# A decoder layer on one core: the query halves of twelve cross-attention tiles, moved from the feed-forward phase to the end of the self attention

## The chip, the cores and the metric

The kernel runs on one core of one Trainium2 chip. The core has a matrix engine (TensorE, "PE" in the profile, with "PEld" for its weight loads), a vector engine (DVE), an activation engine (ACT), a general engine (POOL, also GpSimd) and a sync engine (SP) that here only issues transfers. Each engine takes its instructions from its own queue in order and waits on semaphores for the others. The metric is the device time of one execution in microseconds (us). Three runs of the kernel before took 3417.92, 3418.64 and 3423.78 us, so the median is 3418.64 us.

## The reference, cut to what matters

The layer is a pre-norm decoder: self attention, cross attention and a feed-forward part that itself contains a grouped-query attention and a mixture of experts. `x` has four sequences of 512 tokens with 512 channels, all in float32.

```python
x = x + L0_attn(layernorm(x))          # gated delta rule, 16 heads of 128, causal convolutions
x = x + L0_xattn(layernorm(x), ctx)    # cross attention to 256 context rows, 16 heads of 32
x = x + L0_ffn(layernorm(x))           # 16 query heads, 4 key heads, then 8 experts, 2 per token
```

The change touches the second line:

```python
def L0_xattn(x, cond):
    q = (x @ Wq + bq).reshape(1, B * N, H, hd)
    k, v = ...                                   # of cond @ Wkv + bkv
    q = fq_sym(q * scale, axis=-1)               # round to 255 levels, one step per token and head
    k = fq_sym(k, axis=-1); v = fq_sym(v, axis=2)
    attn = softmax(einsum('bhqd,bhkd->bhqk', q, k))
    attn = fq_unsigned(attn, axis=-1)            # 256 levels, one step per row
    out = einsum('bhqk,bhkd->bhqd', attn, v)
    return out @ Wp + bp
```

## The kernel before, in words

**Tiles.** The 2048 tokens are 16 tiles of 128 rows (`NT`), four to a sequence (`TB`). The self attention works by groups `m` of two heads of one sequence, 32 in all; the later parts work by token tile.

**Streams.** Nearly everything is written as Python generators. A generator issues a few instructions and yields. `turns` (L192) steps several streams round by round, each by a given number of steps; `chain` puts streams one after another; `within` stops a stream for now when the turn is over; `idle(n)` yields n times. So the order in which instructions are written comes from how streams are stepped against each other. In the self attention, DVE, ACT and POOL execute exactly in that written order (L1066, `manual_schedule`); the order on TensorE and of the transfers on SP is chosen by the framework's scheduler, with the written order as priority. After the self attention the scheduler chooses for all engines.

**Self attention.** Turn `m` runs `stage3(m)` (L829), which joins the blocks of an inverse (four steps: L843 to L877) and then runs the recurrence over four chunks: `r` (DVE, L897), `u` (TensorE L904, ACT L906), new state (TensorE L914, DVE L919), output (L922, L924). That makes 15 steps. Each step of it steps the other streams of the turn once or twice: `stage1(m+2)` (keys and queries two groups ahead), `stage2_values(m+1)` (convolutions), the inversion by POOL (L747, L748, 31 rounds) and `output(m-1)` (the projection of the group before, L968). In the last two turns, 30 and 31, there is no stage 1 left, and in turn 31 no convolutions and no inversion either. When `stage3` is through, what is left of the other streams is run off.

**Cross attention of tile i** has two halves. `front(i)` (L244 to L280) loads the tile's rows `x1d` (after self attention) into `xi`, normalizes them (DVE L140, L141, L131, then a power on POOL L132, then DVE L146), transposes them (TensorE L215, copied by ACT L217), projects them (L259, eight matmul instructions), adds the bias (DVE L261), quantizes them (`levels`, seven DVE instructions, L225 to L232; the step per head stays in `x_step`), transposes the bfloat16 levels, stores them in DRAM (`x_q_d`), and reads them back in four transfers with each head's rows three times (`x_qT`, L279). That is 11 steps, or 9 where `xi` was loaded ahead. `back(i)` (L283) makes scores for four heads at a time (L296), their maxima and exponentials (DVE L300 to L302, ACT L306), rounds them (DVE L312), transposes them (L322), weights the values (`weighted`, L328) and projects the result (L364): 14 steps, four scores and roundings, four transposes, two `weighted`.

**Where the halves run.** In turn 30 the streams `front(0)` and `front(1)` start, one step per step of `stage3`; front 0 is done in it. In turn 31 the stream `seam`, two steps at a time, finishes front 1 beside back 0 and continues with `cross(1)`, which is front 2 and back 1. Back 1 gets as far as its second scores. The rest of it runs in the seam (L1606) beside `output(31)` and `norms(0)`.

**The weave.** From there `weave` (L155) merges four kinds of streams by due times: `attention(i)`, `qkv(i)` (projections with weights streamed from DRAM, L1253), `crossing(i)` and `rest_of(i)`. Of all streams, the one whose time is earliest is stepped, and its time advances by its length divided by its expected number of steps (`steps`, L152). `crossing(i)`, for i from 2 to 15, is the norm of tile i-1 beside the first six steps of `cross(i)`, and then the rest of it; `cross(i)` (L370) is front i+1 and then back i. Its streams have due times 3.1 tiles ahead (`X`) with a length of 1.03 (`W`). After the weave the expert blocks run.

**Memory.** The pool `wx` (name `b_x`) holds what both halves of the cross attention need, with single buffers for `xi`, `xn` and `x_qi`; `wz` (`b_v`) is opened in turn 31. The pool `second` is closed at the start of turn 31, and only then the keys and weights of back (`x_kT`, `wpj`, `bp`, `x_val`) are loaded on SP (L1099 to L1104).

Of the kernel before, what the change touches and what calls it, by code (L numbers as in the profile page):

```python
# [31 lines left out]
F32 = mybir.dt.float32  # L32
BF16 = mybir.dt.bfloat16
# [6 lines left out]
P = 128  # L40
# [64 lines left out]
def decoder(ctx: ExitStack, tc: tile.TileContext, a: dict, out: bass.AP):  # L105
# [42 lines left out]
    def chain(*gs):  # L148
        for g in gs:
            yield from g  # L150

    steps = {"first_o": 3, "cross": 30, "qkv": 12, "rest_of": 4, "route": 10, "load": 26}  # L152
    steps.update((f"attention{c}", n) for c, n in enumerate((37, 41, 53, 57)))
# [24 lines left out]
    def idle(n):  # L178
        for _ in range(n):
            yield  # L180
# [6 lines left out]
    def within(g, turn):  # L187

        while turn and next(g, g) is not g:
            yield  # L190
# [45 lines left out]
    x_kT_d, x_val_d = dram.tile([P, 3, KD, M], BF16, name="x_kT_d"), dram.tile([P, 2, D], BF16, name="x_val_d")  # L236
    x_q_d = dram.tile([NT, P, KD, P], BF16, name="x_q_d")

    ao = ctx.enter_context(tc.tile_pool(name="a_o", bufs=2))
    top = ctx.enter_context(ExitStack())  # L240

    hTs, x2s, xis, fronts = {}, {}, {}, {}

    def front(i):  # L244

        xi = xis.pop(i, None)
        if xi is None:
            xi = wx.tile([P, D], F32, name="xi", bufs=1)
            nc.sync.dma_start(xi, x1d[i])
            yield  # L250
            yield
        xn = wx.tile([P, D], F32, name="xn", bufs=1)
        yield from layernorm(xn.unsqueeze(1), xi.unsqueeze(1), wx)
        yield
        xT = transposed(xn, wx, "xT")
        yield
        pq = p_b.tile([P, D], F32, name="pb")
        for kd in range(KD):
            nc.tensor.matmul(pq, xT[:, kd, :], wq[:, kd, :], start=kd == 0, stop=kd == KD - 1)  # L259
        q = wx.tile([P, D], F32, name="xn", bufs=1)  # L260
        nc.vector.tensor_tensor(q, pq, bq, ALU.add)  # L261
        yield
        qi = wx.tile([P, D], BF16, name="x_qi", bufs=1)
        step = wx.tile([P, H2], F32, name="x_step")
        levels(qi, q, step, H2, HD2, wx, float(1.0 / np.sqrt(np.float32(HD2))))
        yield
        yield
        t = transposed(qi, wx, "x_qi", 1)
        yield

        nc.sync.dma_start(x_q_d[i], t)
        if 1 < i + 1 < NT:
            xis[i + 1] = wx.tile([P, D], F32, name="xi", bufs=1)
            nc.sync.dma_start(xis[i + 1], x1d[i + 1])
        yield
        qT = wx.tile([3 * HD2, KD, 4, P], BF16, name="x_qT")
        for r in range(4):
            q = x_q_d[i, r * HD2 : (r + 1) * HD2].unsqueeze(0).to_broadcast([3, HD2, KD, P])
            nc.sync.dma_start(qT[:, :, r, :], q)  # L279
        yield  # L280
        fronts[i] = qT, step

    def back(i):  # L283

        qT, step = fronts.pop(i)
        aT = wx.tile([P, KD, P], F32, name="xT")
# [62 lines left out]
        for u in range(5):  # L349
            if i == 0 and u < KD:  # L350
                nc.gpsimd.tensor_scalar(wpj[:, u, :], wpj[:, u, :], x_sv[:, u : u + 1], None, ALU.mult)
            if u == 3:
                x2 = wz.tile([P, D], F32, name="x2", bufs=2)
                nc.sync.dma_start(x2, x1d[i])
            if u < 4:
                yield from scores(u // 2 * 2, u % 2 * 2, es)
            if u > 0:
                yield from turned(es.pop(0), eTs)
            if u in (2, 4):
                yield from weighted(u - 2, eTs)  # L360
                eTs.clear()
# [6 lines left out]
        x2s[i] = x2  # L368

    def cross(i):  # L370
        return chain(front(i + 1), back(i)) if i + 1 < NT else back(i)


    with ExitStack() as st:
# [707 lines left out]
        for m in range(NP):  # L1082
            rest, turn = [], [0]
            if m == NP - 2:
# [5 lines left out]
                wx = top.enter_context(tc.tile_pool(name="b_x", bufs=2, side="right", reuse_waits="tile"))  # L1090
                fronts_of = chain(idle(2), front(0), front(1))
                rest.append((within(fronts_of, turn), 1))
            if m == NP - 1:
# [11 lines left out]
                wz = top.enter_context(tc.tile_pool(name="b_v", bufs=2, side="right", reuse_waits="tile"))  # L1105
                seam = chain(turns((fronts_of, 1), (chain(idle(3), back(0)), 1)), cross(1))
                rest.append((within(seam, turn), 2))
# [30 lines left out]
    with ExitStack() as st:  # L1138
# [38 lines left out]
        def norms(i):  # L1177


            x2 = x2s.pop(i)  # L1180
            x3 = wq_.tile([P, D], F32, name="x3", bufs=1)
# [404 lines left out]

        at_x = [(2 - X + (i - 2) * W, W, crossing(i), "cross") for i in range(2, NT)]
        for n, t in enumerate((-0.6, 0.2, 1.0)):
            at_x[n] = (t, 0.8, *at_x[n][2:])
        at_x[-1] = (*at_x[-1][:2], last(chain(at_x[-1][2], norms(NT - 1))), "cross")  # L1590
        at_q = [(i - Q, 1.0, qkv(i), "qkv") for i in range(NT)]
# [5 lines left out]
        for i in range(NT - 1):  # L1597
# [172 lines left out]
```

## Time and profile before

| | us |
|---|---|
| median of three runs | 3418.64 |
| the profiled execution | 3410.54 |
| its span (first to last instruction) | 3408.8 |
| busy: TensorE | 3207.6 (94%) |
| busy: DVE | 1831.8 (54%) |
| busy: ACT | 1606.2 (47%) |
| busy: POOL | 1448.0 (42%) |
| turn 30 begins (its first L843) | 1752.8 |
| turn 31 begins (its first L843) | 1798.3 |
| `output(31)` begins after the last `og` | 1872.7 |
| first matmul of `qkv(0)` (L1253) | 1906.9 |
| last matmul of the feed-forward attention (L1359) | 3130.7 |

The stages of the self attention before turn 30 and the weave take nearly the whole span. Busy times are sums over one engine; matmuls are pipelined and their ends are modelled, so the time that a group of matmuls takes is read from the start of the first to the start of what follows. The mean granted TensorE clock of the execution was 0.976 of full speed. In the rows of the timeline, the bracket at the end of a line is how long the engine was idle before it, and what ended that.

### The profile page before, as it was taken

How to read it: one execution, taken by the hardware profiler on the slowest of the kernel's cores; microseconds unless marked ns; L12 is line 12 of the kernel's file. 1: busy time of each engine (PE TensorE's matmuls, PEld its weight loads, DVE VectorE, ACT ScalarE, POOL GpSimd, SP SyncE). 2: the span in 40 equal slices, each digit the busy share in tenths (PEclk: the TensorE clock that was granted, in tenths of full speed). 3: DMA queues.
4: the chain of work that ended last, by engine and by line, in shares of the span. 5: the costliest groups of instructions: out<-in, count | busy, mean ns of one | idle time of the engine just before them, and what ended most of it. 6: DMA issues, size and time to landing. Idle time of an engine off the chain costs nothing. (4 is left out here: it accounts for less than half of the span.)

```text
span 3408.8 us, 48178 instructions
## 1 busy us (share of the span) xinstructions
PE 3207.6 (94%) x16031; PEld 1796.9 (53%) x16031; DVE 1831.8 (54%) x4160; ACT 1606.2 (47%) x4384; POOL 1448.0 (42%) x2768
## 2 busy tenths in 40 slices
PE   5899999999999999999997799999998999899996
PEld 3455555555555555555554355555554555454443
DVE  5755564555645555554554466666655665545111
ACT  3445555455545555445543445555544455534221
POOL 1156756667576675766761221112112111212442
PEclk8999999999999999999997899999999999999998
DMA  6443444534345353444532565556545554556544
GB/s 173 114 122 111 136 109 124 161 114 134 111 124 152 113 147 104 125 138 122 141 98 75 194 201 178 160 176 182 170 158 159 189 164 148 169 164 225 93 81 95
DMA packets 491288, 482.05 MB, mean 141 GB/s; under 512 B 224911, under 2 KB 340117, under 8 KB 490848
## 3 DMA queue, kind: packets, MB, share of 16 engines
q1 hardware_dynamic: 477696, 448.79, 44.2%
q0 software_dynamic: 11904, 27.34, 3.9%
q8 instruction: 128, 2.10, 0.3%
q10 hardware_dynamic: 1440, 2.84, 0.3%
q14 instruction: 120, 0.98, 0.1%
HBM read 416.18 MB, written 66.90 MB: 142 GB/s over the span
## 5 line engine op out<-in xcount | busy, mean ns | idle before, releaser
L594 PE MATMUL pb<-xnT,w 128*128 128x512 f32 x2048 | 958.0, 603 | 0.1
L594 PEld LDWEIGHTS pb<-xnT,w 128*128 128x128 f32 x2048 | 364.1, 192 | 337.2 <-issue 330.7
L605 DVE SCALAR_TENSOR_TENSOR cv<-pb,pp,cv 128x510 f32<-128x510 f32 (+2 forms) x576 | 424.3, 746 | 98.8 <-ACT cv L602 85.6
L748 POOL TENSOR_TENSOR iT<-iT,iW 64x126 f32<-64x126 f32 (+22 forms) x930 | 343.3, 369 | 72.9
L1253 PE MATMUL pb<-c_q,hT 128*128 128x512 f32 x768 | 354.4, 599 | 5.0 <-DMA c_q<-in_c_wq_dram 3.8
L747 POOL TENSOR_TENSOR iW<-iA,iT 64x126 f32<-64x126 f32 (+22 forms) x930 | 319.7, 344 | 65.7 <-issue 0.2
L968 PE MATMUL pb<-wot,og 128*128 128x512 f32 x512 | 248.3, 608 | 11.3 <-ACT x_e L306 6.3
L1172 POOL TENSOR_TENSOR rope_s<-q,tab 128x128 f32<-128x128 f32 x80 | 43.1, 538 | 477.1 <-DVE q L1283 392.2
L1253 PEld LDWEIGHTS pb<-c_q,hT 128*128 128x128 f32 x768 | 141.7, 192 | 156.9 <-issue 146.7
L602 ACT ACTIVATE cv<-pb,pp 128x512 f32<-128x512 f32 x192 | 148.5, 773 | 147.6 <-PE pb L594 143.6
L649 POOL TENSOR_TENSOR rk<-ss,mhalf 128x8 f32<-128x8 f32 x32 | 77.9, 2435 | 277.0 <-DVE ss L648 277.0
L973 DVE TENSOR_TENSOR xa<-pb,xa 128x512 f32<-128x512 f32 x112 | 76.9, 688 | 188.1 <-PE pb L968 188.1
L306 ACT ACTIVATE x_e<-pb,nm,x_step 128x256 f32<-128x256 f32 x256 | 141.1, 565 | 70.2 <-DVE nm L302 60.6
L1349 PE MATMUL po<-eT,val 128*128 128x512 f32 x320 | 165.6, 614 | 7.6 <-ACT eT L1347 4.7
L1359 PE MATMUL pw<-wot,oT 128*128 128x512 f32 x344 | 163.9, 601 | 0.4 <-DVE oT L1351 0.2
L1319 PE MATMUL pb<-kT,qT 128*128 128x256 f32 (+3 forms) x576 | 161.9, 409 | 0.0
L701 POOL TENSOR_TENSOR qg<-qh,row 128x512 f32<-128x512 f32 x64 | 83.2, 1300 | 177.7 <-ACT qh L608 154.8
L968 PEld LDWEIGHTS pb<-wot,og 128*128 128x128 f32 x512 | 92.8, 192 | 106.4 <-issue 88.0
L1660 PE MATMUL pb<-w_gu,eT 128*128 x312 | 141.9, 598 | 2.0 <-issue 2.0
L608 ACT ACTIVATE qh<-cv 128x512 f32<-128x512 f32 x64 | 40.4, 631 | 214.0 <-DVE cv L605 206.1
L132 POOL TENSOR_TENSOR rms_r<-rsq,mhalf 128x1 f32<-128x1 f32 x48 | 27.4, 571 | 243.9 <-DVE rsq L131 243.8
L1347 ACT COPY eT<-pb 128x512 f32<-128x512 f32 x160 | 89.4, 592 | 82.9 <-PE pb L1345 80.1
(389 smaller groups left out, 6184.1 us busy)
## 6 DMA issues: line engine op xcount, KB each, us to landing
c_q<-in_c_wq_dram SPq DMA_DIRECT2D x128, 512.0 KB
w<-in_a_w_dram SPq DMA_DIRECT2D x124, 512.0 KB
wot<-in_c_wo_dram SPq DMA_DIRECT2D x86, 512.0 KB
row<-g_d SPq DMA_DIRECT2D x64, 512.0 KB
c_o<-in_c_wo_dram SPq DMA_DIRECT2D x42, 512.0 KB
at_d<-at SPq DMA_DIRECT2D x64, 256.0 KB
T<-t_d SPq DMA_DIRECT2D x32, 512.0 KB
X<-x_d SPq DMA_DIRECT2D x32, 512.0 KB
```

What stands on the lines that cost most here:

```text
L306: nc.scalar.activation(e[:, 2 * r + g, :], ps[r][:, g, :], AF.Exp, bias=nm[:, r, g : g + 1], scale=step[:, h : h + 1], accum_out=ssum[:, g ...
L594: nc.tensor.matmul(pj, wt[:, kd, p * P : (p + 1) * P], xnT[:, kd, :], start=kd == 0, stop=kd == KD - 1)
L602: nc.scalar.activation(ac, pj, AF.Identity, bias=cb[:, m, h : h + 1], scale=cw[:, m, h, 3:4])
L605: nc.vector.scalar_tensor_tensor(ac[:, j:], pj[:, : S - j], cw[:, m, h, 3 - j : 4 - j], ac[:, j:], ALU.mult, ALU.add)
L747: eng.tensor_tensor(u, A[:, i, i + 1 :].unsqueeze(2).to_broadcast([nb, n, w]), T[:, i, :w].unsqueeze(1).to_broadcast([nb, n, w]), ALU.mult)
L748: eng.tensor_tensor(T[:, i + 1 :, :w], T[:, i + 1 :, :w], u, ALU.add)
L968: nc.tensor.matmul(pw, og[p][:, c * P : (c + 1) * P], wot[:, p, :], start=p == 0, stop=p == HG - 1)
L1253: nc.tensor.matmul(pj, hT[:, kd, :], w[:, kd % 2, :], start=kd == 0, stop=kd == KD - 1)
L1319: nc.tensor.matmul(ps[:, m, k * P : (k + w) * P], qT[g][:, n + m, :], kT[:, g, j : j + w, :], start=True, stop=True)
L1349: nc.tensor.matmul(po, val[:, g, :], eT, start=k == 0, stop=k == c)
L1359: nc.tensor.matmul(pw, oT[:, h + m, :], w[:, m, :], start=g == 0 and h + m == 0, stop=g == 3 and h + m == 3)
L1660: nc.tensor.matmul(pg, hT[:, kd, :], w_gu[:, bass.ds(e, 1), kd, :, :], start=kd == 0, stop=kd == KD - 1)
```

## The change

The fronts of tiles 0 to 11 no longer run in the weave. Tiles 0, 1, 2, 4, 5, 7, 8, 9, 10 and 11 form one stream, `fronts_of`, which is stepped twice per step of `stage3` in turns 30 and 31 and once per round in the seam, until it ends. Fronts 3 and 6 are streams of their own, in turn 30 and in turn 31, with a small pool each (`x_more`). A front of `fronts_of` loads the next front's rows once its own are normalized, so all but the first have 8 steps in place of 11.

A front now ends by storing its levels in `x_q_d` and its steps in a new DRAM tensor `x_s_d`. Reading them back is a new function, `fetch`, with the four transfers of before and one for the steps. `back(i)` calls it for tile i+1 at its third part if that front is done, or at its own start for tile i. `x_qT` moves from the pool `wx` to `wz`.

The seam stream is only back 0 and back 1, two steps per step of `stage3` in turn 31. In the weave, `crossing(2)` to `crossing(10)` and `crossing(15)` hold only the back (kind "back", 20 steps expected); `crossing(11)` to `crossing(14)` hold fronts 12 to 15 as before. `norms(i)` waits until tile i's cross attention is written.

```diff
-    steps = {"first_o": 3, "cross": 30, "qkv": 12, "rest_of": 4, "route": 10, "load": 26}
+    steps = {"first_o": 3, "cross": 30, "back": 20, "qkv": 12, "rest_of": 4, "route": 10, "load": 26}
...
-    x_q_d = dram.tile([NT, P, KD, P], BF16, name="x_q_d")
+    x_q_d, x_s_d = dram.tile([NT, P, KD, P], BF16, name="x_q_d"), dram.tile([NT, P, H2], F32, name="x_s_d")
...
-    def front(i):
-
-        xi = xis.pop(i, None)
-        if xi is None:
-            xi = wx.tile([P, D], F32, name="xi", bufs=1)
-            nc.sync.dma_start(xi, x1d[i])
+    def front(i, pool=None, then=None):
+        pool = pool or wx
+
+        def load(n):
+            xis[n] = pool.tile([P, D], F32, name="xi", bufs=1)
+            nc.sync.dma_start(xis[n], x1d[n])
+
+        if i not in xis:
+            load(i)
             yield
             yield
...
+        if then is not None:
+            load(then)
...
         nc.sync.dma_start(x_q_d[i], t)
-        if 1 < i + 1 < NT:
-            xis[i + 1] = wx.tile([P, D], F32, name="xi", bufs=1)
-            nc.sync.dma_start(xis[i + 1], x1d[i + 1])
+        nc.sync.dma_start(x_s_d[i], step)
+        fronts.add(i)
         yield
-        qT = wx.tile([3 * HD2, KD, 4, P], BF16, name="x_qT")
+
+    def fetch(i):
+        qT = wz.tile([3 * HD2, KD, 4, P], BF16, name="x_qT")
         for r in range(4):
             q = x_q_d[i, r * HD2 : (r + 1) * HD2].unsqueeze(0).to_broadcast([3, HD2, KD, P])
             nc.sync.dma_start(qT[:, :, r, :], q)
-        yield
-        fronts[i] = qT, step
+        step = wz.tile([P, H2], F32, name="x_step")
+        nc.sync.dma_start(step, x_s_d[i])
+        queries[i] = qT, step

     def back(i):

-        qT, step = fronts.pop(i)
+        if i not in queries:
+            fetch(i)
+            yield
+            yield
+        qT, step = queries.pop(i)
...
+            if u == 2 and i + 1 in fronts:
+                fetch(i + 1)
...
+    AHEAD = 3 * TB
+
     def cross(i):
-        return chain(front(i + 1), back(i)) if i + 1 < NT else back(i)
+        return chain(front(i + 1), back(i)) if AHEAD <= i + 1 < NT else back(i)
...
-                fronts_of = chain(idle(2), front(0), front(1))
-                rest.append((within(fronts_of, turn), 1))
+                more = second.enter_context(tc.tile_pool(name="x_more", bufs=1))
+                mine = (0, 1, 2, 4, 5, 7, 8, 9, 10, 11)
+                fronts_of = chain(idle(2), *(front(i, None, then) for i, then in zip(mine, (*mine[1:], None))))
+                rest.append((within(fronts_of, turn), 2))
+                rest.append((chain(idle(4), front(3, more)), 1))
...
-                seam = chain(turns((fronts_of, 1), (chain(idle(3), back(0)), 1)), cross(1))
+                more = st.enter_context(tc.tile_pool(name="x_more", bufs=1))
+                rest.append((chain(idle(2), front(6, more)), 1))
+                rest.append((within(fronts_of, turn), 2))
+                seam = chain(back(0), back(1))
                 rest.append((within(seam, turn), 2))
...
+            while i not in x2s:
+                yield
             x2 = x2s.pop(i)
...
-        at_x = [(2 - X + (i - 2) * W, W, crossing(i), "cross") for i in range(2, NT)]
+        at_x = [(2 - X + (i - 2) * W, W, crossing(i), "cross" if AHEAD <= i + 1 < NT else "back") for i in range(2, NT)]
...
-        run(turns((output(NP - 1), 1), (norms(0), 1), (seam, 1)))
+        run(turns((output(NP - 1), 1), (norms(0), 1), (seam, 1), (fronts_of, 1)))
```

More of the change, by code (lines that the diff above doesn't have):

```diff
@@ L236, in decoder @@
     x_kT_d, x_val_d = dram.tile([P, 3, KD, M], BF16, name="x_kT_d"), dram.tile([P, 2, D], BF16, name="x_val_d")
-    x_q_d = dram.tile([NT, P, KD, P], BF16, name="x_q_d")
+    x_q_d, x_s_d = dram.tile([NT, P, KD, P], BF16, name="x_q_d"), dram.tile([NT, P, H2], F32, name="x_s_d")
     ao = ctx.enter_context(tc.tile_pool(name="a_o", bufs=2))
     top = ctx.enter_context(ExitStack())
-    hTs, x2s, xis, fronts = {}, {}, {}, {}
-    def front(i):
-        xi = xis.pop(i, None)
-        if xi is None:
-            xi = wx.tile([P, D], F32, name="xi", bufs=1)
-            nc.sync.dma_start(xi, x1d[i])
+    hTs, x2s, xis, queries, fronts = {}, {}, {}, {}, set()
+    def front(i, pool=None, then=None):
[5 more added lines that the diff above has]
+            load(i)
             yield
             yield
-        xn = wx.tile([P, D], F32, name="xn", bufs=1)
-        yield from layernorm(xn.unsqueeze(1), xi.unsqueeze(1), wx)
+        xi = xis.pop(i)
+        xn = pool.tile([P, D], F32, name="xn", bufs=1)
+        yield from layernorm(xn.unsqueeze(1), xi.unsqueeze(1), pool)
         yield
-        xT = transposed(xn, wx, "xT")
+        if then is not None:
+            load(then)
+        xT = transposed(xn, pool, "xT", 2 if pool is wx else 1)
         yield
@@ L259, in front @@
             nc.tensor.matmul(pq, xT[:, kd, :], wq[:, kd, :], start=kd == 0, stop=kd == KD - 1)
-        q = wx.tile([P, D], F32, name="xn", bufs=1)
+        q = pool.tile([P, D], F32, name="xn", bufs=1)
         nc.vector.tensor_tensor(q, pq, bq, ALU.add)
         yield
-        qi = wx.tile([P, D], BF16, name="x_qi", bufs=1)
-        step = wx.tile([P, H2], F32, name="x_step")
-        levels(qi, q, step, H2, HD2, wx, float(1.0 / np.sqrt(np.float32(HD2))))
+        qi = pool.tile([P, D], BF16, name="x_qi", bufs=1)
+        step = pool.tile([P, H2], F32, name="x_step")
+        levels(qi, q, step, H2, HD2, pool, float(1.0 / np.sqrt(np.float32(HD2))))
         yield
         yield
-        t = transposed(qi, wx, "x_qi", 1)
+        t = transposed(qi, pool, "x_qi", 1)
         yield
         nc.sync.dma_start(x_q_d[i], t)
-        if 1 < i + 1 < NT:
-            xis[i + 1] = wx.tile([P, D], F32, name="xi", bufs=1)
-            nc.sync.dma_start(xis[i + 1], x1d[i + 1])
+        nc.sync.dma_start(x_s_d[i], step)
+        fronts.add(i)
         yield
-        qT = wx.tile([3 * HD2, KD, 4, P], BF16, name="x_qT")
+    def fetch(i):
+        qT = wz.tile([3 * HD2, KD, 4, P], BF16, name="x_qT")
         for r in range(4):
@@ L1585, in decoder @@
         Q, X, W = 1.36, 3.1, 1.03
-        at_x = [(2 - X + (i - 2) * W, W, crossing(i), "cross") for i in range(2, NT)]
+        at_x = [(2 - X + (i - 2) * W, W, crossing(i), "cross" if AHEAD <= i + 1 < NT else "back") for i in range(2, NT)]
         for n, t in enumerate((-0.6, 0.2, 1.0)):
             at_x[n] = (t, 0.8, *at_x[n][2:])
-        at_x[-1] = (*at_x[-1][:2], last(chain(at_x[-1][2], norms(NT - 1))), "cross")
+        at_x[-1] = (*at_x[-1][:2], last(chain(at_x[-1][2], norms(NT - 1))), "back")
         at_q = [(i - Q, 1.0, qkv(i), "qkv") for i in range(NT)]
```

## The prediction

> **What bounds the kernel now.** I read the page first for the share of each engine and for where in the span it changes, then the busy time by stage around the change, then the order of instructions and the waits inside those stages. Part 2 of the page, 40 slices of 85 us, TensorE and its granted clock:
>
> ```profile
> PE   5899999999999999999997799999998999899996
> PEclk8999999999999999999997899999999999999998
> ```
>
> TensorE is full nearly everywhere, except in slices 22 and 23 (1790 to 1960 us): the last two turns of the self attention and the seam. The busy time by stage shows it sharper. The stages are cut at the first matmul of turn 30, of turn 31, of `output(31)`, at the first projection of the feed-forward attention (L1253), and at 1960 us, after which the weave runs evenly; columns are TensorE, its weight loads, DVE, ACT and POOL, granted clock, DMA share, GB/s:
>
> ```profile
> core 0: us, PE busy (x) PEld busy (x) DVE busy (x) ACT busy (x) POOL busy (x), PEclk, DMA share, GB/s
> 1752.80:1798.30 45.50, 39.58 (x237) 23.81 (x236) 19.84 (x39) 12.74 (x34) 25.20 (x53) 0.92 0.36 103
> 1798.30:1872.70 74.40, 50.76 (x313) 31.07 (x312) 38.55 (x88) 28.63 (x83) 16.11 (x16) 0.78 0.27 80
> 1872.70:1906.90 34.20, 22.86 (x112) 11.87 (x113) 17.72 (x46) 13.04 (x34) 9.99 (x14) 0.67 0.68 237
> 1906.90:1960.00 53.10, 42.04 (x188) 22.21 (x187) 26.53 (x66) 24.22 (x68) 10.12 (x17) 0.87 0.51 161
> 1960.00:3125.00 1165.00, 1123.41 (x4731) 612.00 (x4730) 701.44 (x2003) 587.72 (x1566) 207.63 (x313) 0.99 0.56 178
> ```
>
> The weave is bound by TensorE: 1123.4 of 1165 us (96%) at clock 0.99, DVE at 60%. Turn 31 is bound by nothing: TensorE idles 23.6 us, DVE 35.9 us. There a chain over engines sets the pace, since DVE, ACT and POOL take their work strictly in the written order. One passage of front 0 in turn 30 shows what that costs. TensorE, from the timeline:
>
> ```profile
> 1770.44 0.60 PE L215 MATMUL pb<-tab,xn 128*128 128x128 f32 x4
> 1770.88 1.88 PE L594 MATMUL pb<-xnT,w 128*128 128x512 f32 x4
> ...
> 1773.04 3.60 PE L259 MATMUL pb<-wq,xT 128*128 128x512 f32 x8
> 1776.47 0.61 PE L914 MATMUL ps<-u,kdec 128*128 128x128 f32 x4
> ...
> 1784.64 0.80 PE L904 MATMUL ps<-r,X 128*128 128x128 f32 x2 [4.77 <-DVE r L897]
> ```
>
> and DVE in the same stretch:
>
> ```profile
> 1776.68 0.69 DVE L261 TENSOR_TENSOR xn<-pb,bq 128x512 f32<-128x512 f32 x1 [5.65 <-PE pb L259]
> ...
> 1779.24 0.68 DVE L225 TENSOR_REDUCE x_step<-xn 128x16 f32<-128x512 f32 x1
> ...
> 1783.24 0.43 DVE L232 TENSOR_SCALAR x_qi<-xn 128x512 bf16<-128x512 f32 x1
> ...
> 1784.24 0.60 DVE L897 SCALAR_TENSOR_TENSOR r<-ps,ngam,vn 128x128 f32<-128x128 f32 x2
> ```
>
> DVE first waits 5.65 us for the projection, then works off the quantization (`levels`), and only then the recurrence's `r`; TensorE stands 4.77 us for it. In turn 31 the DVE waits repeat the pattern (us in total, times, longest):
>
> ```profile
> DVE xn L261 <- PE pb L259: 10.4, 2, 7.3
> DVE x_ei L312 <- ACT x_e L306: 5.7, 3, 2.4
> DVE ln_st L140 <- DMA xi<-x1d: 4.4, 2, 2.7
> ```
>
> **What a front costs.** TensorE, by starts: 0.44 (f32 transposes, 1770.44 to 1770.88) + 3.43 (projection, 1773.04 to 1776.47) + 0.42 (bf16 transposes) = 4.29 us. DVE by the medians of its lines: 0.69 + 0.18 + 0.15 + 0.55 + 0.69 + 0.69 + 0.17 + 0.25 + 0.17 + 0.69 + 0.43 + 0.43 = 5.09 us. ACT: two copies of 0.58. POOL: one power of 0.55.
>
> **Weave.** Fronts 3 to 11 leave it, nine: 9 x 4.29 = **-38.6 us**. It stays bound by TensorE, as DVE loses work too. Bounds: -40 (divided by 96%) and -25, if its 41.6 us of idle grow by a third because the fronts no longer fill them.
>
> **Turn 30.** It carries front 0 now; by counting steps (two per step of `stage3`, one for front 3) it will carry 0, 1, 2 and 3. Three more: 12.9 us of TensorE. The turn has 5.9 us of TensorE idle, so at least +7. At most each new front also stalls the recurrence by 4.8 us as front 0 did: 12.9 + 14.3 = +27. Their `levels` fall in steps 4, 10 and 12, apart from each other, with step 8 stalling as now; so I take two stalls less a few us of filled idle: 12.9 + 9.5 - 2.4 = **+20**. POOL gets three more powers among the inversion's pairs (0.85 us a pair). The inversion ended at 1779.6 and its loads were issued by 1783.2 for a use at 1798.3, so 15 us cover that; without them it would cost 1.7.
>
> **Turn 31.** It carries fronts 1 and 2, back 0 and two scores of back 1. After: fronts 4 to 8, back 0, and back 1 but for its projection. DVE adds 3 x 5.1 for fronts, and for back 1 another 7.1 (two scores of 1.6, three roundings of 0.69, two `weighted` of 0.9): +22.4 us. Lowest is 0, since new TensorE work (12.9 + 3.9 = 16.8) is less than the 23.6 idle. Highest: the DVE work in full, three waits for projections at their mean (5.2) and three for exponentials (2.4): 22.4 + 15.6 + 7.3 = +45. The row nearest is the turn's own start, where a front and a back ran together: the inverse's steps started at 1801.6, 1813.9 and 1822.1, 10 us a step, against 4.2 where only back 0 ran (1822.1 to 1847.2, six steps). After the change all 15 steps carry both. So I lie near the top: 22.4 + 3 x 3.08 (the smaller projection wait) + 2 x 2.4 = **+36**. On SP, tile 0's queries are now fetched in turn 31, behind `x_kT` (6.14 us of issuing), `wpj`, `bp` and `x_val`: last of four issued about 1811.3, landed some 2.7 us later (as `xi`, issued 1852.57, was used at 1855.25), 2.4 us after the first scores ran now (1811.6); DVE and ACT stand behind those scores. That lies in the 36. In POOL the power of front 5 stands behind the scaling of `wpj` (6.2 us now), again inside the bounds.
>
> **Seam, 1872.7 to 1906.9.** TensorE holds 22.9 us at clock 0.67. Back 1 leaves all but its projection (3.9 us less); fronts 9 to 11 come (12.9) and fill idle time. The stage ends when the first projection's weights, issued from 1877.5 on, are in and TensorE is past back 1. DMA runs at 0.84 to 0.92 up to 1900, so at most 10 us can go: **-6**, bounds -10 and +13 (no cover at all). In 1906.9 to 1960 TensorE idles 11.1 us, partly behind back 1 and tile 1's norm, which come earlier: **-2**, bounds -11 and 0.
>
> **Steps through DRAM.** Each tile gains a store and a load of 8 KB, each about 0.33 us of SP issue (as the 4 KB `r_d` store, 0.32), beside 6.14 us for the query's loads that were there. SP has gaps; nothing on the path: 0. If the cover went, 0.7 x 16 = 11 us. [...]
>
> **Sum.** 20 + 36 - 6 - 2 - 38.6 = **+9.4 us**. The profiled execution took 3410.54 us (span 3408.8 and 1.7 around it), 8 under the median of three runs, 3418.64; it would become 3419.9, and the median **3428.0**.
>
> The granted clock could give back more: 0.78 in turn 31, 50.8 us busy, so at most 50.8 x 0.22 = 11 us. I take none, since the waits of 2.4 to 7.3 us remain. [...]
>
> **Rivals.** With G the growth of both turns (56 forecast), the time is 3418.6 + G - 46.6.
> - *Fronts fill idle TensorE.* For it: 29.5 us idle in the two turns, and fronts of two pools that overlap. Against: the waits are DVE's, in order. Its bound, G = 7, gives 3379; around G = 22, 3394. It decides below G = 40: faster by over 0.2%.
> - *Even.* G of 40 to 53: 3412 to 3425, within 0.2% (6.8 us, about what a measurement of this kernel can tell from no change).
> - *The weave gives back less.* TensorE waits there for `x_ei` (6.8), `h` (6.5) and `c_q` (3.8); if the missing fronts leave holes (-25 for -38.6): 3442, with G at its bound of 72, 3458.
> - *The change does nothing*, since TensorE's work is only moved: 3418.6. The stages differ too much in their idle time for more than chance to make it even; it counts within the even case.
>
> **Numbers.** Forecast case, G 53 to 75, 3425 to 3447: 0.43. Fill: 0.28. Even: 0.17. Less back, above 3447: 0.12. So faster 0.28, same 0.17, slower 0.55. The range 3396 to 3450 leaves out about a tenth at each end.
>
> **What would show it.** Turn 30 (from the first L843 of group 30 to that of group 31) at 65 us and turn 31 at 110; TensorE waiting there for `r`, `x_ei` and `xn`; clock still under 0.9. First L1253 about 28 us after `og`. The weave from there to the last L1359 shorter by 35 to 40 us. I am wrong if the turns grow by less than 40 us, or if the weave keeps its length.

## The result, and the profile after

The change made the kernel slower: 3448.88 us (median of 4 runs, 3445.81 to 3451.13) against 3418.47 us (4 runs, 3417.92 to 3423.78), a ratio of 1.0085 with a 95% interval of 1.0067 to 1.0102, or +30.4 us. Forecast were +9.4 us, a median of 3428.0 and a range of 3396 to 3450. The profiled execution after took 3445.81 us, span 3444.0.

Part 2 of the page of the changed kernel, TensorE in 40 slices of 86 us; the dip stands where it stood before, in slices 22 and 23, and is no shallower:

```profile
PE   5899999999999999999997699999998999899996
```

The busy time by stage of the changed kernel, cut at the first matmul of turn 30, of turn 31, of `output(31)` (1934.26), at the first projection of the encoder (L1281, L1253 before) and at the last `L1387` (L1359 before):

```profile
core 0: us, PE busy (x) PEld busy (x) DVE busy (x) ACT busy (x) POOL busy (x), PEclk, DMA share, GB/s
1756.30:1816.80 60.50, 52.67 (x285) 29.43 (x284) 35.14 (x78) 15.96 (x40) 27.67 (x57) 0.97 0.30 90
1816.80:1934.30 117.50, 73.23 (x438) 44.29 (x437) 58.31 (x136) 41.60 (x114) 16.50 (x17) 0.77 0.27 73
1934.30:1981.30 47.00, 32.49 (x84) 15.38 (x85) 25.17 (x67) 6.03 (x13) 13.29 (x19) 0.79 0.54 185
1981.30:3163.60 1182.30, 1137.15 (x4791) 618.23 (x4789) 683.12 (x1965) 602.25 (x1616) 212.25 (x320) 0.99 0.57 180
```

The last three of these stages in the kernel before, on the same marks (its first `output(31)` matmul is at 1873.83, which moves that cut by 1.1 us against the prediction's):

```profile
1798.30:1873.80 75.50, 50.76 (x313) 31.07 (x312) 39.65 (x89) 29.73 (x87) 16.11 (x16) 0.78 0.27 79
1873.80:1906.90 33.10, 22.86 (x112) 11.87 (x113) 16.62 (x45) 11.94 (x30) 9.99 (x14) 0.68 0.69 243
1906.90:3130.70 1223.80, 1171.02 (x4934) 636.87 (x4933) 729.85 (x2072) 612.19 (x1633) 217.75 (x330) 0.99 0.56 177
```

So the stages compare as follows:

| stage, us | before | after | difference | forecast |
|---|---|---|---|---|
| turn 30 | 45.5 | 60.5 | +15.0 | +20 |
| turn 31 | 75.5 | 117.5 | +42.0 | +36 |
| seam | 33.1 | 47.0 | +13.9 | -6 |
| woven stretch | 1223.8 | 1182.3 | -41.5 | -40.6 |
| seam and woven stretch together | 1256.9 | 1229.3 | -27.6 | -46.6 |

Before turn 30 and after the weave the two executions differ by another 5.8 us. The start of turn 30 alone lay between 1753.1 and 1756.8 us in kernels that are the same up to there, so these are not counted.

TensorE's idle time tells it most shortly. In turn 31 the kernel before idled 24.7 us (75.5 less 50.76); the changed one, with five fronts and most of back 1 in it, idles 44.3 (117.5 less 73.23). The added work did not go into the idle time, it brought more along. In seam and weave together TensorE idled 63.0 us before (10.2 and 52.8) and 59.7 after (14.5 and 45.2), so little idle time was filled there either. The waits of TensorE in turn 31 of the changed kernel (us in total, times, longest):

```profile
PE pb L352 <- DVE x_by L349: 7.9, 3, 4.1
PE pb L267 <- ACT xT L217: 5.1, 2, 4.2
PE pb L215 <- ACT x_e L321: 5.1, 2, 2.6
PE pb L311 <- DMA x_qT<-x_q_d: 5.0, 2, 3.3
PE pb L988 <- DVE og L955: 4.8, 1, 4.8
PE po L942 <- ACT u L926: 3.8, 1, 3.8
```

There is no one cause: backs (L352), fronts (L267, L215), the fetched queries (L311) and the recurrence (L942, L988) take turns in being late. VectorE waits the other way round, for TensorE's projections (10.4 us before) and for ScalarE's exponentials (5.7 us before):

```profile
DVE xn L269 <- PE pb L267: 22.0, 5, 7.8
DVE x_ei L327 <- ACT x_e L321: 13.0, 5, 3.8
```

The seam is where the forecast had the wrong sign. TensorE's timeline of the changed kernel from the second `output(31)` part on:

```profile
1947.07 3.60 PE L267 MATMUL pb<-wq,xT 128*128 128x512 f32 x8
1950.51 0.60 PE L1224 MATMUL pb<-tab,h 128*128 128x128 f32 x4
...
1956.80 0.61 PE L215 MATMUL pb<-ident_i,x_qi 128*128 128x128 bf16 x4 [4.91 <-DVE x_qi L232]
1957.47 1.09 PE L215 MATMUL pb<-tab,xn 128*128 128x128 f32 x4
1959.23 5.15 PE L267 MATMUL pb<-wq,xT 128*128 128x512 f32 x8 [0.68 <-ACT xT L217]
1968.30 0.40 PE L215 MATMUL pb<-ident_i,x_qi 128*128 128x128 bf16 x4 [3.92 <-DVE x_qi L232]
...
1970.80 6.18 PE L267 MATMUL pb<-wq,xT 128*128 128x512 f32 x8 [0.68 <-ACT xT L217]
1980.91 0.61 PE L215 MATMUL pb<-ident_i,x_qi 128*128 128x128 bf16 x4 [3.92 <-DVE x_qi L232]
1981.31 4.58 PE L1281 MATMUL pb<-c_q,hT 128*128 128x512 f32 x5
```

Fronts 9, 10 and 11 go one after the other, about 12 us apart (1947.07, 1959.23, 1970.80), each a bare chain: projection, then VectorE's quantization, then the bf16 transposes for which TensorE stands 4 to 5 us. The first projection of the encoder needs `hT`, whose transposes are at 1950.51, and weights whose loads were issued by 1940.6. It could start then (in kernel 10 below it starts at 1951.04), but it stands in TensorE's queue behind all three fronts, until 1981.31.

### The profile page after: what moved, and what is told of

Its sections match the earlier page's. It is cut to its first block, busy times and chain, and to the rows that moved or that the text cites. A ratio compares the mean times of both kernels' runs of the same rounds, so it can differ in the third digit from the quotient of the medians.

```text
span 3444.0 us, 48299 instructions
## 1 busy us (share of the span) xinstructions
PE 3222.1 (94%) x16031; PEld 1802.1 (52%) x16031; DVE 1827.7 (53%) x4160; ACT 1606.3 (47%) x4384; POOL 1452.3 (42%) x2768
## 5 line engine op out<-in xcount | busy, mean ns | idle before, releaser
L1281 PE MATMUL pb<-c_q,hT 128*128 128x512 f32 x768 | 356.6, 603 | 6.8 <-DVE q L1297 4.1
L988 PE MATMUL pb<-wot,og 128*128 128x512 f32 x512 | 249.5, 611 | 9.8 <-DVE og L955 4.8
L1281 PEld LDWEIGHTS pb<-c_q,hT 128*128 128x128 f32 x768 | 142.4, 193 | 160.8 <-issue 146.4
L1387 PE MATMUL pw<-wot,oT 128*128 128x512 f32 x344 | 164.2, 605 | 6.1 <-DVE oT L1379 6.0
L988 PEld LDWEIGHTS pb<-wot,og 128*128 128x128 f32 x512 | 93.2, 193 | 105.2 <-issue 94.3
```

The costliest lines, as they stand in the source:

```text
L988: nc.tensor.matmul(pw, og[p][:, c * P : (c + 1) * P], wot[:, p, :], start=p == 0, stop=p == HG - 1)
L1281: nc.tensor.matmul(pj, hT[:, kd, :], w[:, kd % 2, :], start=kd == 0, stop=kd == KD - 1)
L1387: nc.tensor.matmul(pw, oT[:, h + m, :], w[:, m, :], start=g == 0 and h + m == 0, stop=g == 3 and h + m == 3)
```

## The experiments

Each was timed against the kernel before on its own chip; the ratio is to that. Stages are those of one profiled execution, in us. They vary from kernel to kernel where nothing was changed: turn 31 takes 117.5 and 119.9 us in the changed kernel and in kernel 10, which are written alike up to its end; seam and weave take 1228.5 to 1231.6 us in the five kernels that share them with the changed one (changed, 6, 7, 11, 12). So a difference of some 3 us in one stage says nothing.

| kernel | median | ratio [95%] | turn 30 | turn 31 | seam and weave |
|---|---|---|---|---|---|
| before | 3418.5 | 1 | 45.5 | 75.5 | 1256.9 |
| changed | 3448.9 | 1.0085 [1.0067, 1.0102] | 60.5 | 117.5 | 1229.3 |
| 1: no fronts at the seam | 3444.9 | 1.0071 [1.0054, 1.0088] | 62.1 | 120.0 | 1224.2 |
| 2: no fronts in turn 31 | 3432.1 | 1.0039 [1.0025, 1.0053] | 61.8 | 80.8 | 1249.8 |
| 3: changed, order freed | 3443.4 | 1.0068 [1.0051, 1.0084] | 72.5 | 102.4 | 1231.2 |
| 4: before, order freed | 3421.8 | 1.0009 [0.9999, 1.0018] | 58.1 | 60.6 | 1264.5 |
| 5: queries of tile 0 early | 3432.6 | 1.0044 [1.0028, 1.0060] | 61.9 | 73.3 | 1255.1 |
| 6: fronts 4-8 without quantization | 3436.7 | 1.0044 [1.0027, 1.0061] | 61.9 | 109.4 | 1231.6 |
| 7: fronts 4-8, quarter projection | 3436.7 | 1.0047 [1.0030, 1.0065] | 60.8 | 107.5 | 1228.5 |
| 8: front 0 only | 3434.8 | 1.0042 [1.0028, 1.0056] | 41.8 | 58.9 | 1298.4 |
| 9: before, projection at the seam | 3411.6 | 0.9987 [0.9978, 0.9996] | 46.2 | 75.9 | 1256.1 |
| 10: changed, projection at the seam | 3447.0 | 1.0096 [1.0080, 1.0111] | 60.3 | 119.9 | 1229.6 |
| 11: changed, TensorE kept busy | 3445.5 | 1.0086 [1.0071, 1.0102] | 62.2 | 121.5 | 1229.0 |
| 12: fronts 4-8 with neither | 3427.3 | 1.0024 [1.0014, 1.0033] | 60.5 | 98.1 | 1229.6 |

**1. What the fronts at the seam cost.**

```diff
-    AHEAD = 3 * TB
+    AHEAD = 9
-                mine = (0, 1, 2, 4, 5, 7, 8, 9, 10, 11)
+                mine = (0, 1, 2, 4, 5, 7, 8)
```

> Fronts 9, 10 and 11 go back into the woven stretch; everything else stays as in the changed kernel. Theory (the first projection of the encoder waits in TensorE's queue behind the fronts that run at the seam): the seam, 47.0 us in the changed kernel, falls to 28 to 31 us, the woven stretch grows by 3 fronts of 4.29 us (12.9 us), turns 30 and 31 keep their 60.6 and 117.4 us (turn 31 may lose a few us if front 9 began in it); sum 3442 to 3446 us on the profiled 3445.8. Rival (the projection waits for its own data at the seam, the weights or the output transposes, and the fronts only fill that wait): the seam stays above 42 us, the woven stretch grows all the same, sum about 3455 to 3461 us.

The sum came out as the theory had it (3444.9), but not by its stages. Seam and weave of this kernel:

```profile
1938.20:1952.30 14.10, 14.06 (x36) 6.74 (x37) 8.28 (x29) 2.56 (x7) 7.85 (x10) 0.82 0.81 305
1952.30:3162.40 1210.10, 1153.77 (x4838) 626.89 (x4838) 699.91 (x2002) 605.08 (x1624) 215.97 (x329) 0.98 0.57 179
```

The seam fell by 33 us, not by 17, and the weave grew by 28, not by 13: the first projection is only a mark in TensorE's queue, and what comes before or after it shifts with the order. So seam and weave have to be taken together. Together they are 5.1 us shorter without the three fronts at the seam, although the three fronts' 12.9 us of TensorE are then back in the weave. So the three cost 18 us at the seam, 6 us each, in a place where the forecast had them hidden; at the price of a front in the weave that kernel 2 gives below (5.1 us), it is 20.5 us, or 6.8 each. TensorE's idle time in the two stages agrees: 56.4 us here, 59.7 with the fronts at the seam. The whole runs cannot tell the two kernels apart (the intervals of 1.0071 and 1.0085 overlap), and the turns of this profiled execution read 4.1 us longer.

**2. What the fronts in turn 31 cost.**

```diff
-    AHEAD = 3 * TB
+    AHEAD = 4
-                mine = (0, 1, 2, 4, 5, 7, 8, 9, 10, 11)
+                mine = (0, 1, 2)
...
-                rest.append((chain(idle(2), front(6, more)), 1))
-                rest.append((within(fronts_of, turn), 2))
```

> Only fronts 0 to 3 run ahead: 0 to 2 in one stream, 3 in its own beside it, begun in turn 30; turn 31 keeps back 0 and the start of back 1 with their queries through DRAM; the other eight go back into the woven stretch. Theory (the fronts put into turn 31 are what lengthens it, each with its own chain through VectorE's written order): turn 31 falls from 117.4 us to 65 to 75 us, the seam to 25 to 31 us, the woven stretch grows by 8 fronts of 4.29 us = 34 us, turn 30 stays at about 60 us; sum 3410 to 3425 us. Rival (the trip of queries and steps through DRAM, or back 1 brought forward, lengthens turn 31): turn 31 stays at 95 us or more, sum 3445 to 3465 us.

Turn 31 fell to 80.8 us: far from the rival's 95, 6 us above the theory's 75, and the sum 7 us above the theory's highest. Against kernel 1, which differs from this one by five fronts: turn 31 grows by 39.2 us (120.0 less 80.8), 7.8 a front, and seam and weave shrink by 25.6, 5.1 a front. That makes 13.6 us, about half of the 29.4 by which the stages of the changed kernel are longer than before. The other half is in kernel 2 already: by its stages it is 14.5 us longer than the kernel before (turn 30 +16.3, turn 31 +5.3, seam and weave -7.1), with no front left in turn 31 and only front 3 taken out of the weave. What makes it is not separated: fronts 1 and 2 now run in turn 30, and most of back 1 runs in turn 31, where tile 0's queries come back from DRAM. A wait of TensorE for these queries is the longest there:

```profile
PE pb L311 <- DMA x_qT<-x_q_d: 10.2, 2, 8.7
```

With no front to do, TensorE stands 10.2 us for them; in the changed kernel it was 5.0, and front 4's projection ran (1822.12 to 1827.44) in the time ahead of them.

**3 and 4. The written order of VectorE, ScalarE and GpSimd.** The same edit in the changed kernel and in the one before:

```diff
-        st.enter_context(tc.manual_schedule(engines={...}))
+        written = st.enter_context(ExitStack())
+        written.enter_context(tc.manual_schedule(engines={...}))
...
             if m == NP - 2:
+                written.close()
                 first.close()
```

> The changed kernel, with the written order of VectorE, ScalarE and GpSimd given up from turn 30 on: the compiler's scheduler orders them there. Theory (the waits of turn 31 come from the order in which the streams' small VectorE steps stand in the queue: each waits at the head of it for a result of its own chain, with steps of other streams that are ready behind it): turn 31 falls from 117.4 us by 20 us or more, the sum to 3400 to 3428 us. Rival (the streams' total work, the lower granted clock and late transfers set the length of turn 31, not the order): turn 31 within 8 us of 117.4, the sum 3435 to 3455 us. The freed order could also make the seam longer, which would show in the seam alone.

> The kernel before with the same order freed from turn 30 on, as the counterpart of the other. By the theory of the order there are fewer streams to stand behind each other, so turns 30 and 31 (45.5 and 75.5 us) change by less than 8 us each and the sum stays at 3405 to 3425 us; by the rival likewise. Where this kernel gains as much as the changed one does, the order is a fault of both and says nothing about the growth of turn 31.

Turns 30 and 31 of the changed kernel with the freed order:

```profile
1756.30:1828.80 72.50, 52.64 (x289) 29.96 (x291) 33.45 (x79) 15.92 (x40) 27.34 (x57) 0.86 0.26 75
1828.80:1931.20 102.40, 67.68 (x437) 39.97 (x437) 57.39 (x150) 42.89 (x117) 21.77 (x23) 0.80 0.31 82
```

and of the kernel before:

```profile
1754.50:1812.60 58.10, 40.72 (x238) 24.00 (x237) 19.94 (x46) 12.71 (x34) 26.18 (x55) 0.82 0.28 80
1812.60:1873.20 60.60, 40.24 (x314) 25.09 (x313) 36.78 (x94) 27.62 (x77) 20.49 (x19) 0.94 0.43 126
```

Both did the same: turn 30 longer by 12 us, turn 31 shorter by 15, and the two together shorter by only 3.1 and 2.3 us. Neither expectation for a single turn held, in the kernel before either. The order decides in which turn the time falls; the growth by 57 us (121.0 to 178.0) stays, at 56 (118.7 to 174.9). So the order as written is not the cause, and my theory of it fell. What the two runs do not test is order as such: the scheduler too writes one order for each engine.

**5. Tile 0's queries fetched in turn 30.** Their room was that of front 3's tiles, so front 3 went back into the weave:

```diff
+    def early(i):
+        fetch(i)
+        yield
...
-        qT = wz.tile([3 * HD2, KD, 4, P], BF16, name="x_qT")
+        qT = wx.tile([3 * HD2, KD, 4, P], BF16, name="x_qT")
...
+                fronts_of = chain(idle(2), fronts_of[0], early(0), *fronts_of[1:])
-                rest.append((chain(idle(4), front(3, more)), 1))
```

> As the kernel with only fronts 0 to 3 ahead (3432.1 us; turn 30 61.8, turn 31 80.8 us), but front 3 goes back into the woven stretch and in the room of its tiles the queries and step of tile 0 are fetched in turn 30, where the changed kernel fetches them at the start of turn 31. Theory (the trip of tile 0's queries through DRAM is on the path: TensorE stood 10.2 us for them in turn 31): turn 31 falls from 80.8 to 70 to 73 us, turn 30 from 61.8 to 54 to 58 us (one front less), the seam and the woven stretch together grow from 1249.8 to 1254 or 1255 us; sum 3414 to 3425 us. Rival (the wait is only exchanged for the next one, the exponentials of back 0 and back 1): turn 31 stays at 78 us or more, sum 3426 to 3433 us.

Turn 31 fell to 73.3 us as expected, and seam and weave grew to 1255.1. Turn 30 kept its 61.9 us with one front less in it, where 54 to 58 were expected, and the median is that of kernel 2 (3432.6 and 3432.1; the profiled execution, 3426.0, was the fastest of five). So of the 7.5 us that turn 31 lost, front 3 took 5.3 back in the weave, and turn 30 did not give its part. In turn 30 TensorE now stood 5.81 us for one front's `x_qi`. In turn 31 it no longer stood for the queries, but 4.1 us for `x_kT`. The fetch alone does not seem to lengthen turn 30: kernel 8, which has it there beside front 0 only, takes 41.8 us for it, less than the kernel before.

**6, 7 and 12. Which engine's work sets turn 31.** Fronts 4 to 8 without quantization (6), with a quarter of the projection (7), with neither (12):

```diff
+        if 4 <= i <= 8:
+            nc.vector.tensor_tensor(qi, pq, bq, ALU.add)
+            nc.vector.memset(step, 1.0)
...
+        K = 1 if 4 <= i <= 8 else KD
+        for kd in range(K):
```

> The changed kernel, but fronts 4 to 8 leave out the quantization of their queries (the queries are rounded to bf16 unscaled, the step is set to 1): 2.83 us of VectorE less for each, 14.2 us in all, TensorE's work as it was. Theory A (VectorE, which takes its work in the written order, sets the length of turn 31): turn 31 falls from 117.5 us by 10 us or more, sum 3430 to 3440 us. Theory B (TensorE's own work sets it, the fronts' matmuls being added whole and at the lower clock): turn 31 falls by 4 us or less, sum 3444 to 3450 us.

> The changed kernel, but fronts 4 to 8 leave out three of the four accumulating matmuls of their projection: 2.6 us of TensorE less for each at full clock, 3.3 us at the 0.77 granted in turn 31, 13 to 17 us in all; VectorE's work as it was. Theory B (TensorE's own work sets the length of turn 31): it falls from 117.5 us by 12 us or more, sum 3430 to 3437 us. Theory A (VectorE's written order sets it, TensorE has idle time to spare): it falls by 5 us or less, sum 3443 to 3450 us.

> The changed kernel, with both left out of fronts 4 to 8: the quantization (14.2 us of VectorE) and three of the four matmuls of the projection (13 to 17 us of TensorE). Left out singly, they shortened turn 31 from 117.5 us by 8.1 and by 10.0 us. Theory (both lie one behind the other on the chain that sets the turn, so that what each saves is added): turn 31 falls by 16 to 20 us, to 98 to 101 us, sum 3422 to 3430 us. Rival (each alone already removes the same waits, since one stands for the other): it falls by 12 us or less, sum 3432 to 3438 us.

Turn 31 of kernel 6, of kernel 7 and of kernel 12 (TensorE, weight loads, VectorE, ScalarE, GpSimd, clock, DMA):

```profile
1818.50:1927.90 109.40, 71.88 (x438) 42.18 (x437) 43.65 (x107) 41.50 (x114) 17.05 (x18) 0.80 0.27 74
```

```profile
1817.00:1924.50 107.50, 59.41 (x407) 37.74 (x407) 57.02 (x136) 41.59 (x114) 16.50 (x17) 0.76 0.30 80
```

```profile
1817.30:1915.40 98.10, 60.02 (x408) 38.34 (x407) 43.61 (x107) 41.45 (x114) 17.54 (x18) 0.75 0.31 84
```

Kernel 6 has 14.7 us of VectorE less (58.31 to 43.65) and is 8.1 us shorter; kernel 7 has 13.8 us of TensorE less and is 10.0 us shorter: between theories A and B, each of which would have had one of them at nothing. Kernel 12 is 19.4 us shorter, about the sum of both (18.1), as its theory had it. So the two works lie one behind the other on what sets the turn: some 55 and 72 parts in a hundred of what was left out, on VectorE and on TensorE, were paid for. VectorE's waits for the projections show where (kernel 6 in two rows, then kernel 7; 22.0 in the changed kernel):

```profile
DVE x_qi L271 <- PE pb L267: 18.0, 4, 7.7
DVE x_qi L271 <- issue: 8.6, 1, 8.6
DVE xn L270 <- PE pb L268: 10.2, 3, 4.4
```

In kernel 7 VectorE waits 11.8 us less for the projections, and the turn is 10.0 us shorter: a projection is paid for as VectorE's wait for it. In kernel 6 VectorE has 14.7 us less to do, but idles 6.6 more (65.8 for 59.2), 4.6 of it in front of the bias, which waits for the projections (18.0 and 8.6 for 22.0; the one of 8.6 also ends as a projection does, at 1830): part of the time freed turns into waiting.

**11. TensorE kept busy at its waits.**

```diff
         pq = p_b.tile([P, D], F32, name="pb")
+        if 4 <= i <= 8:
+            for _ in range(2):
+                nc.tensor.matmul(pq, wq[:, 0, 0:P], wq[:, 0, :], start=True, stop=True)
...
             ts = p_b.tile([P, 2, P], F32, name="pb")
+            if i < 2:
+                for _ in range(4):
+                    nc.tensor.matmul(ts.rearrange("p g d -> p (g d)"), wq[:, 0, 0:P], wq[:, 0, 0 : 2 * P], start=True, stop=True)
```

(and three such ahead of tile 0's first scores)

> The changed kernel with matmuls added in front of those for which TensorE stood waiting in turn 31, their results overwritten by the real ones: two 128x512 ahead of each projection of fronts 4 to 8, four 128x256 ahead of each reciprocal turned over in backs 0 and 1, three 128x512 ahead of tile 0's first scores: 21 us of TensorE at full clock in all, of which 17 us lie at waits of the profile. Theory (the low granted clock of turn 31, 0.77, comes from TensorE's short waits, and its longer matmuls are part of what the fronts cost there): the clock of turn 31 rises to 0.87 or more and the turn gets no longer than 117.5 us in spite of the added work, sum 3440 to 3449 us. Rival (the clock does not follow, or the added work delays what is on the path): the clock below 0.82 and turn 31 longer by 8 us or more, sum 3456 to 3470 us.

```profile
1815.90:1937.40 121.50, 89.83 (x495) 53.51 (x495) 57.19 (x135) 41.74 (x114) 16.71 (x17) 0.83 0.27 71
```

16.6 us more of TensorE (89.83 against 73.23) lengthened the turn by 4.0 us, little more than the spread, and the whole not measurably (1.0086 against 1.0085). The clock rose from 0.77 to 0.83, less than the theory's 0.87; the rival's (under 0.82, 8 us or more) did not come either. The faster clock reached the fronts' own matmuls, as the rows of their projections show (changed kernel, then kernel 11):

```profile
L267 PE MATMUL pb<-wq,xT 128*128 128x512 f32 x40 | 21.8, 696 | 5.2 <-ACT xT L217 5.1
L270 PE MATMUL pb<-wq,xT 128*128 128x512 f32 x40 | 18.3, 600 | 0.0
```

They were busy 3.5 us less in all, but the added matmuls stand ahead of them, and VectorE's wait for the projections grew from 22.0 to 25.1 us. So what the clock alone is worth is not separated here from the price of the added work; together they won nothing. Matmuls at waits cost 4.0 us for 16.6, while a front's matmuls were paid for at 72 parts in a hundred (kernel 7): what counts in turn 31 is whether work lies on the chain. With these matmuls the clock was higher (0.83 for 0.77) and the turn longer, so that any of the 11 us that the prediction put on the clock at most can be had is not shown.

**8. Only front 0 ahead.** The edit is against kernel 5:

```diff
-                mine = (0, 1, 2)
+                mine = (0,)
-                seam = chain(back(0), back(1))
+                seam = chain(idle(3), back(0), front(1), cross(1))
```

> As the kernel with early queries, but only front 0 runs ahead; fronts 1 and 2 run after back 0, in turn 31's last part or at the seam, the others in the woven stretch. Theory (a front costs more in turns 30 and 31 than the woven stretch gives back for it, so the fewer run there the better): turns 30 and 31 at 45 to 48 and 60 to 70 us, the seam and the woven stretch together 1263 to 1268 us, sum 3412 to 3424 us. Rival (after back 0 the two fronts are bare chains of 11.5 us each, as fronts 10 and 11 were at the seam of the changed kernel): the seam and the woven stretch 1272 us or more, sum 3428 to 3440 us.

The rival held in its numbers, not in its reason. The two turns took 100.7 us, 20.3 less than before, but seam and weave 41.5 more. What TensorE's timeline of this kernel shows bare at the seam is not the two fronts but back 1, alone from 1871 to 1911, waiting for its queries and for the rounding of its exponentials (`x_ei`):

```profile
1877.64 0.61 PE L316 MATMUL pb<-x_kT,x_qT 96*128 96x256 bf16 x2 [5.37 <-DMA x_qT<-x_q_d]
1881.32 0.61 PE L316 MATMUL pb<-x_kT,x_qT 96*128 96x256 bf16 x2 [3.07 <-DMA x_qT<-x_q_d]
1886.69 1.03 PE L342 MATMUL pb<-ident_i,x_ei 128*128 128x128 bf16 x8 [4.76 <-DVE x_ei L332]
...
1910.64 7.03 PE L1282 MATMUL pb<-c_q,hT 128*128 128x512 f32 x16
```

**10 and 9. The first projection beside what runs at the seam.** In the changed kernel (10; 11 steps) and in the one before (9; 6 steps):

```diff
+        def beside():
+            while 0 not in hTs:
+                yield
+            yield from idle(1)
+            yield from itertools.islice(q0, 11)
...
-        run(turns((output(NP - 1), 1), (norms(0), 1), (seam, 1), (fronts_of, 1)))
+        run(turns((output(NP - 1), 1), (norms(0), 1), (seam, 1), (fronts_of, 1), (beside(), 1)))
```

> The changed kernel, but the first projection of the encoder and its norms and turnings (11 of its 12 steps) are written between fronts 9 to 11 at the seam, from the step after tile 0's norm on, where the changed kernel has them behind all three fronts in TensorE's queue. Theory (the three fronts cost 18 us at the seam instead of hiding there, since nothing that is ready stands between their steps): the seam and the woven stretch together fall from 1229.3 to 1211 to 1221 us, sum 3431 to 3441 us on a median of 3448.9. Rival (the first projection's weights, or the work of tile 0's norms, come no earlier, and the fronts are longer for the company): 1226 us or more, sum 3445 to 3452 us.

> The kernel before, with the first six of the twelve steps of the first projection written beside back 1 at the seam in the same way. Theory (TensorE's idle time at the seam, 10.2 of 33.1 us, can be filled by work that is next in line anyway): the seam and the woven stretch together fall from 1256.9 to 1247 to 1253 us, sum 3409 to 3416 us against 3419 of the kernel before. Rival (back 1 is delayed by as much as the projection gains, its last part being the next that the projection of tile 1 waits for): 1255 to 1262 us, sum 3417 to 3426 us.

In the changed kernel the seam filled as meant, and seam and weave still took 1229.6 us. The busy time of kernel 10 in stretches of 10 us shows what took its place:

```profile
1970.00:1980.00 10.00, 10.00 (x33) 4.93 (x32) 5.98 (x15) 2.35 (x5) 2.65 (x5) 1.00 0.90 334
1980.00:1990.00 10.00, 5.74 (x23) 3.15 (x22) 5.66 (x16) 3.33 (x8) 3.16 (x6) 0.80 0.65 212
1990.00:2000.00 10.00, 6.14 (x20) 3.19 (x19) 5.37 (x12) 0.59 (x1) 0.00 (x0) 0.67 0.09 30
2000.00:2010.00 10.00, 5.12 (x44) 3.30 (x43) 5.43 (x17) 8.47 (x27) 0.55 (x1) 0.50 0.07 25
2010.00:2020.00 10.00, 5.73 (x30) 3.52 (x28) 4.55 (x12) 5.90 (x17) 0.00 (x0) 0.50 0.19 38
```

and its timeline, what TensorE stands for there:

```profile
1987.43 6.34 PE L267 MATMUL pb<-wq,xT 128*128 128x512 f32 x8 [1.77 <-ACT xT L217]
1997.62 0.61 PE L215 MATMUL pb<-ident_i,x_qi 128*128 128x128 bf16 x4 [3.86 <-DVE x_qi L232]
...
2004.69 1.03 PE L337 MATMUL pb<-ident_i,x_ei 128*128 128x128 bf16 x8 [3.89 <-DVE x_ei L327]
```

The projection went first, and then front 11 and back 2 ran bare, at little over half of TensorE: it idles 17.3 us from 1980 to 2020. In the changed kernel it idles 13.6 us from 1950 to 1980 and 5.0 from 2010 to 2020. The hole moved by 30 us and about kept its size: there is one projection to put beside several chains, and it can be used once. My theory that a better place for the projection would win back the seam fell, and the time (3447.0) lies where the rival had it.

In the kernel before the same edit won a little: 3411.62 us (11 runs) against 3415.9 on that chip (15 runs), a ratio of 0.9987 [0.9978, 0.9996], faster than both kernels, though by less than the 0.2% taken above as a measurable difference. The profiled execution, at 3413.6 one of the slower ones, does not show where: its seam and weave are 1256.1 us against 1256.9, on the rival's side (1255 to 1262) and not the theory's (1247 to 1253). That the gain comes from the seam is therefore not shown.

## Why the prediction was right and where it was wrong

- **Direction and bound.** Slower was the likeliest case, and the time lies in the range, but only by 1 us of its upper end and in the case above 3447, which had a chance of 0.12. The growth of the turns, G, was 57.0 us against 56 forecast; with it the prediction's own formula gives 3418.6 + 57.0 - 46.6 = 3429. Of the other 20 us, 19 are in the term -46.6.
- **Turn 30, +20: near in size**, +15.0, but not by the stalls. The forecast added to TensorE's 12.9 us two stalls of the recurrence, less 2.4 of filled idle time. TensorE's work grew by 13.1 us (39.58 to 52.67), its idle time by only 1.9 (5.9 to 7.8), and the wait of 4.77 us for `r` that the stalls were modelled on is gone. In its place stand short waits for the fronts themselves:

```profile
PE pb L215 <- DVE xn L146: 3.5, 4, 1.4
PE pb L215 <- DVE x_qi L232: 2.6, 1, 2.6
```

- **Turn 31, +36: right in size**, +42.0, near the top as chosen, and on VectorE by the terms named. Its work grew by 18.7 us (39.65 to 58.31) for 22.4 forecast, its waits for projections by 11.6 (10.4 to 22.0) for 9.2, those for exponentials by 7.3 (5.7 to 13.0) for 4.8: 37.6 us of the 42.0, where the forecast had 36.4. That each of these us lengthens the turn is too much: kernels 6, 7 and 12 show the work of both engines on the path in part, added up. On TensorE the forecast named waits for `r`, `x_ei` and `xn`; these came to 1.9, 0 and 1.3 us, and others took their place. That the order as written was the reason is refuted by kernels 3 and 4.
- **Tile 0's queries, 2.4 us late**, contained in the 36: about right. Before, the first scores started 13.3 us after the turn's first matmul (1811.63); in the changed kernel it is 15.1 (1831.93), 1.8 later, and the next two come 2.1 us after them, where before they followed at once. How long TensorE stood for them (5.0 us, 10.2 in kernel 2) is another number, since it depends on what else TensorE had to do.
- **The seam, -6: wrong, and the step that failed.** It was "fronts 9 to 11 come (12.9) and fill idle time". The stage grew by 13.9 us. Put properly, over seam and weave together, moving these three there from the weave made it 5.1 us longer (kernels 1 and changed) where the forecast counted -12.9: 18 us of the 19 that seam and weave are off. In the terms of the forecast, TensorE's work there was to fall by 29.6 us (six fronts and 3.9 of back 1) and its idle time by 17.0; the work fell by 24.3 and the idle time by 3.3 (63.0 to 59.7). I had taken the idle time of the seam as room. It was the idle time of a chain, and a front is a chain too. The bound of +13 ("no cover at all") counted TensorE's time alone; three bare chains of some 12 us need more.
- **The weave, -38.6 and -2: the number looks right (-41.5) and says little,** as kernel 1 shows how much of it depends on the cut. For fronts 4 to 8, kernels 1 and 2 give 5.1 us a front for the 4.29 counted, so the price of a front in the weave was, if anything, low. By the same terms kernel 1 should have had seam and weave 33.7 us shorter than before (6 x 4.29 + 2 + 6), and it had 32.7; but kernel 2 should have had 12.3 and had 7.1. Taken together, the two give 5.1 us a front and only 2 in all for the terms -6 and -2: in kernel 1 two errors cancel.
- **Steps through DRAM, 0:** no run isolates them. The store took 0.34 us of SP (median) as counted, the load 1.89 in place of the 0.33 counted (least, median and most of the 16 loads, in ns):

```profile
L291 SPq DMA_DIRECT2D x_step<-x_s_d x16: 320/1891/5613, 1833.8 to 2884.8; - x16
```

  VectorE waited 3.2 us once for a step in turn 31, in the same place as for the queries.
- **The clock:** nothing was taken and nothing came, 0.78 to 0.77 in turn 31. The 11 us that it could give back at most were an estimate from 50.8 us busy at 0.78, and no run shows them: in kernel 11, with 16.6 us of work added, the clock was 0.83 and the turn 4.0 us longer. What the kernel before shows at the wait of 4.77 us for `r` is a clock of 0.66 in 1780 to 1790, with nearly all of the wait in it, and of 0.50 from its end (1784.64) to 1789.
- **The rivals.** "Fronts fill idle TensorE" is out: turn 31's idle time grew by 19.6 us. "The weave gives back less" had the right outcome (3442 to 3458) by the wrong place: the weave did not keep holes, the seam did not take the three fronts.
- **The signs.** Turn 30 at 60.5 us (65 forecast), turn 31 at 117.5 (110) and the weave shorter by 41.5 (35 to 40) came about as said; the first projection of the encoder came 47 us after `og` in place of 28, which is the seam again.

What stays open: what makes the 14.5 us that kernel 2 already loses, and why a front in turn 31 is paid for in part and not in full. For the second, TensorE's own queue, the one order that no run freed, is a likely place, since the waits of fronts, backs and recurrence alternate there; that is argued, not shown.

## What to carry to other kernels

Idle time of an engine in a stage that is set by a chain need not be room: here, moved work cost what its own chain added, 7.8 us a front in turn 31 and 6 to 7 at the seam, against the 5.1 that a stage full of matmuls gave back. Whether idle time can be used is tested cheaply: add work to it that depends on nothing (it cost 4.0 us for 16.6), and leave out parts of the moved work engine by engine; savings that add up speak for both engines lying on the chain. Cut stages where a cut does not depend on the order that the change alters, or take neighbouring stages together before a term is called right.

## What the runs showed that was not expected

Half of the loss (14.5 of 29.4 us) was there with a single front out of the weave (kernel 2). Filling waits with matmuls raised the clock of turn 31 from 0.77 to 0.83 and made the fronts' own matmuls faster (696 to 600 ns), with no gain in time. Giving the order of three engines to the scheduler moved 12 us from one turn to the one ahead of it, in two different kernels, with less than 4 us of difference in the two turns' sum.
